# Attention energies in one PSUM bank: one scaled product, two more added on top, one exponential

## The chip, the cores and the metric

The kernel runs on one core of one Trainium2 chip. The time is the device time of one execution in microseconds (us). The kernel before took 2440.59 us (median of three runs, 2437.53 to 2440.74). The engines are PE (TensorE: matmuls and, as PEld, weight loads), ACT (ScalarE), DVE (VectorE), POOL (GpSimd, which here mostly issues DMAs) and SP (SyncE, DMAs too). SBUF is the working memory, PSUM the memory that matmuls write: 8 banks of 2 KB in each of 128 partitions.

## What is computed

Self-attention over the 4096 pixels of each of 4 images with 256 channels, without the softmax's usual subtraction of the maximum (a check of the sums at the end starts a second, general branch that the inputs here do not enter):

```
q = x @ Wq + bq ; k = x @ Wk + bk ; v = x @ Wv + bv
energy[n, m] = sum_c q[c, n] * k[c, m]          # 4096 x 4096 for each image
out[c, n]    = sum_m v[c, m] * softmax_m(energy[n, :])[m]
result       = gamma * out + x
```

The reference is in fp32. The kernel multiplies in a faster matmul type (fp32r), which keeps fewer bits, and gets the precision back by splitting each operand into a rounded upper part and remainders: three products stand for one. For the energies, with E = 2^-12, the three products (forms f = 0, 1, 2) of keys and queries are combined as (1+E)/E times the sum of the products 0 and 1, minus 1/E times product 2, and the exponential of the combination is wanted.

## The kernel before, in words

The work of an image has a **head** and 128 **steps**.

The head (loop over i = 0 to 15) makes the projections of 256 pixels at a time: `transposed` (four transposes on PE, copied out by ACT), `project_qk` (PE, then DVE adds the bias at L144; the keys are split by ACT at L263 and DVE at L266; POOL stores the queries, L275, and the split keys, L279, in DRAM) and `project_v`. From i = 10 on, `begin` slips in the energies of the first three steps, two halves (k = 0, 1) for each step.

A step u covers 512 keys and 256 queries. The order of the instructions on each engine is written out by hand in `tile_conv_attention_kernel` (a manual schedule: each engine runs its own instructions in the order of the program). In step u the program issues:

- `energy(ahead, k)` for the step that lies three ahead (LOOK = 3, ahead = u + 3), for both halves. A half is six matmuls of 128x128 weights (keys) by 256 columns (queries): forms 0 and 1 add up in the tile `sa`, form 2 goes to `sb`; each of the two tiles is one PSUM bank with two buffers. ACT takes the exponential of each (L334) into SBUF tiles `x` and `y`.
- `join(u + 2)`: DVE multiplies x by y (L344), 128x1024 elements.
- `upper(u + 2)`: ACT rounds x to its upper part h (L349). `halves(u + 1)`: DVE makes the remainders l (L355) and d (L358).
- `load_k(ahead + 2)`, L314: POOL issues the DMA of the split keys of step u + 5 (768 KB), into a pool of three buffers (`kpool`, tag "k"). So this load waits until PE has made the energies of step u + 2 out of the same buffer. POOL's other DMAs stand in the same queue: the stores of the head, and the output stores (L436).
- `attend(u)`: 24 matmuls of h, l and d of step u by three forms of the values (L398) into the tiles `a` and `bb`, which are read out every eight steps (`finish`).

So 36 matmuls make a step, 12 for energies and 24 for `attend`. The first loads of keys of an image are issued in `begin`: k_0, k_1 and k_2 at i = 4, 6 and 8, k_3 at i = 13, k_4 at i = 15; k_5 is issued in step 0. Each stands in POOL's queue behind the stores of the i before it. (k_n is the load for step n.)

Four PSUM banks hold energies (`ps_s`), three `a` and `bb` (`ps_o`), one the transposes of the result (`ps_t`).

Of the kernel before, what the change touches and what calls it, by code (L numbers as in the profile page):

```python
# [9 lines left out]
F32 = mybir.dt.float32  # L10
F32R = mybir.dt.float32r
I32 = mybir.dt.int32
AF = mybir.ActivationFunctionType
ALU = mybir.AluOpType
AX = mybir.AxisListType
PSUM = bass.MemoryType.PSUM
# [4 lines left out]
def kernel(  # L21
# [36 lines left out]
    nc = tc.nc  # L58
    B, W, H, C = x.shape
    P = 128  # L60
# [138 lines left out]
    with ExitStack() as fast:  # L199
# [10 lines left out]
        pool("pad3", 1).tile([P, 48], F32, name="pad3")  # L210
        kpool = pool("kpool", 3)
        dram = pool("dram", 2, space=DRAM)
        ps_s = pool("ps_s", 2, space=PSUM)
        ps_o = pool("ps_o", 1, space=PSUM)
        ps_t = pool("ps_t", 1, space=PSUM)

# [8 lines left out]

        images, qd, kf, units, loads, now = [], {}, {}, {}, {}, {}

        energies = cycle((ps_s, tag) for tag in "ab")
        outputs = cycle([(ps_o, "a0"), (ps_o, "a1"), (ps_o, "bb"), (ps_t, "t")])
        active = []  # L230

# [79 lines left out]
        def load_k(b, u):  # L311
            if u < STEPS:
                t = kpool.tile([P, 4, 3, P], F32R, tag="k", name=f"k_{b}_{u}")
                nc.gpsimd.dma_start(t.rearrange("p (i s) f d -> p i s (f d)", s=2), kf[b, u % NU])  # L314
                loads[b, "k", u] = t

        def energy(b, u, k):

            g, t = divmod(u, NU)
            if k == 0:  # L320
                x = ppool.tile([P, 4, NB], F32, tag="x", name=f"x_{b}_{u}", bufs=3)
                y = ppool.tile([P, 4, NB], F32, tag="y", name=f"y_{b}_{u}")
                units[b, u] = x, y
            x, y = units[b, u]
            q, kt = loads[b, "q", g], loads[b, "k", u]
            sa = ps_s.tile([P, 2, NJ, P], F32, tag="a", name=f"sa_{b}_{u}_{k}")
            sb = ps_s.tile([P, 2, NJ, P], F32, tag="b", name=f"sb_{b}_{u}_{k}")
            for i in range(2):
                for to, f, first, last in ((sa, 0, True, False), (sa, 1, False, True), (sb, 2, True, True)):
                    nc.tensor.matmul(  # L330
                        to[:, i], kt[:, 2 * k + i, f, :], q[:, f], start=first, stop=last
                    )
            for to, sp, scale in ((x, sa, (1.0 + E) / E), (y, sb, -1.0 / E)):
                nc.scalar.activation(  # L334
                    to[:, 2 * k : 2 * k + 2, :],
                    sp.rearrange("p i j d -> p i (j d)"),
                    AF.Exp,
                    scale=scale,
                )

        def join(b, u):

            x, y = units[b, u]
            nc.vector.tensor_tensor(x, x, y, ALU.mult)  # L344
            units[b, u] = x

        def upper(b, u):
            h = ppool.tile([P, 4, NB], F32R, tag="h", name=f"h_{b}_{u}", bufs=3)
# [94 lines left out]
        def finish_last(b, g, xr):  # L443

            z = zall.rearrange("p n j -> p (n j)")
            n0 = (b * NG + g) * NJ
            r = work.tile([P, 2, NJ], F32, tag="r", name=f"r_{b}_{g}")
            o = work.tile([P, NJ, C + 2], F32, tag="o", name=f"o_{b}_{g}")
            ok = ppool.tile([P, 4, NB], F32, tag="y", name="ok")
            last = ok[:, 1, : NJ + 1]  # L450
            inside(ok[:, 0, :n0], z[:, :n0])
            nc.vector.tensor_reduce(last[:, NJ:], ok[:, 0, :n0], AX.X, ALU.min)
            acc, bb = now["acc"], now["bb"]
            for j in range(NJ):
                zj, raj = z[:, n0 + j : n0 + j + 1], r[:, 1, j : j + 1]
                nc.vector.tensor_copy(zj, acc[j][:, C : C + 1])
                nc.vector.reciprocal(r[:, 0, j : j + 1], zj)  # L457
                nc.vector.tensor_tensor(raj, r[:, 0, j : j + 1], gam1, ALU.mult)
                nc.scalar.activation(o[:, j, :C], acc[j][:, :C], AF.Identity, scale=raj)
            nc.vector.tensor_tensor(r[:, 0, :], r[:, 0, :], gam.to_broadcast([P, NJ]), ALU.mult)  # L460
            inside(last[:, :NJ], z[:, n0:])

            nc.vector.tensor_reduce(zs, last, AX.X, ALU.min)
            zp = ps_s.tile([P, 1], F32, tag="b", name="zp")
            nc.tensor.matmul(zp, ones, zs, start=True, stop=True)  # L465
            tps = []
            for j in range(NJ):
                nc.vector.scalar_tensor_tensor(  # L468
                    o[:, j, :C], bb[:, j, :], r[:, 0, j : j + 1], o[:, j, :C], ALU.mult, ALU.add
                )  # L470
                tp = (ps_t, ps_s)[j].tile([P, 2, P], F32, tag="ta"[j], name=f"ot_{b}_{g}_{j}")
                for s in range(2):
                    nc.tensor.transpose(tp[:, s, :], o[:, j, s * P : (s + 1) * P], ident)  # L473
                tps.append(tp)
                if j == 0:
                    nc.vector.tensor_scalar(again, zp, P - 0.5, None, ALU.is_lt)
            for j in range(NJ):
                n = slice(j * P, (j + 1) * P)
                nc.vector.tensor_tensor(xr[:, :, n], xr[:, :, n], tps[j], ALU.add)  # L479
            nc.sync.dma_start(ov[b, g], xr)  # L480

        def begin(b, i):

            if i == 5:
                load_q(b, 0)
            if i == 9:
                for _ in halve_q(b, 0):
                    pass
            if i in (4, 6, 8):
                load_k(b, i // 2 - 2)  # L490
            if i >= 10:
                energy(b, (i - 10) // 2, i % 2)
            if i in (12, 14):
                join(b, i // 2 - 6)
            if i in (13, 15):
                upper(b, i // 2 - 6)
                load_k(b, i // 2 - 3)

        image(0)
        for b in range(B):  # L500
            pr = images[b]
            if b == 0:
                now["banks"] = energies
                pr.transposed(0)

                wp = ps_t.tile([P, P], F32, tag="t", name="wp1")
                for _ in range(2):
                    nc.tensor.matmul(wp, ones, ones, start=True, stop=True)
                pr.transposed(1)
                project_qk(b, 0)  # L510
            for i in range(1, NI):
                if i == 3:
                    now["banks"] = outputs
                if i + 1 < NI:
                    pr.transposed(i + 1)
                while i == 1 and active:
                    proceed()
                begin(b, i)
                project_qk(b, i)
                if i == NI - 1:  # L520
                    halves(b, 0)
                project_v(b, i - 1)
                proceed()
            project_v(b, NI - 1)
            for u in range(STEPS):
                g, t = divmod(u, NU)
                ahead = u + LOOK
                if ahead // NU + 1 < NG and ahead % NU == 3:
                    load_q(b, ahead // NU + 1)
                if u == STEPS - NU and b + 1 < B:  # L530
                    image(b + 1)
                if u >= STEPS - 3 and b + 1 < B:
                    now["banks"] = energies
                    if u == STEPS - 3:
                        images[b + 1].load(0)
                    elif u == STEPS - 2:
                        images[b + 1].transposed(0)
                if t == NU - 3:
                    loads[b, "x", g] = load_x(xpool, b, g)


                beside = []
                if ahead // NU + 1 < NG and ahead % NU == 5:
                    beside.append(halve_q(b, ahead // NU + 1))
                if u in (1, 3):
                    beside.append(halve_v(b, NI - 2 + u // 2))
                for k in range(2):
                    if ahead < STEPS:
                        energy(b, ahead, k)
                    if k == 0:  # L550
                        for forms in beside:
                            next(forms)
                    if k == 0 and u + 2 < STEPS:
                        join(b, u + 2)
                        upper(b, u + 2)
                load_k(b, ahead + 2)
                proceed()
                if u + 1 < STEPS:
                    halves(b, u + 1)
                for forms in beside:  # L560
                    next(forms)
                attend(b, u)
                if (b, u) == (B - 1, STEPS - 1):
                    finish_last(b, g, loads.pop((b, "x", g)))
                elif t == NU - 1:
                    start(finish(b, g, now["o"], now["bb"], loads.pop((b, "x", g))))
                proceed()
            if b + 1 < B:
                proceed()
                images[b + 1].transposed(1)  # L570
                proceed()
                project_qk(b + 1, 0)
# [135 lines left out]
```

## Time and profile before

| | |
|---|---|
| runs | 2437.53, 2440.74, 2440.59 us; median 2440.59 |
| span of the profiled execution (first to last instruction) | 2435.2 us, 5.4 below the median of the runs; no other time of that execution is given |
| granted PE clock | 0.999 of full speed |
| ACT exponentials, L334 | 2 x 1024, about 600 ns each |
| DVE multiplication, L344 | 512, 1223 ns each |
| DMA | 498.92 MB, mean 205 GB/s |

The page lists the busy time of each engine, then the costliest groups of instructions, with the mean duration of one and the idle time of the engine just before them. Matmuls overlap in PE's pipeline: a row says 277 ns for one, but successive ones start some 113 ns apart, so the spacing of starts is what counts. A DMA row tells the time from issue to landing. The waits view lists who waited for whom, and the timeline the instructions in order of time.

### The profile page before, as it was taken

The page shows a single profiled execution, that of the slowest core. Times are in us where ns is not written, and L with a number is a line of the kernel's source. Part 1 is how long each engine was busy: PE and PEld are TensorE (multiplying, and loading weights), DVE is VectorE, ACT ScalarE, POOL GpSimd, SP SyncE. Part 2 cuts the span into 40 slices and gives each one's busy share as a digit, 9 for nine tenths or more (in the row PEclk, how much of TensorE's full clock was granted, in tenths as well). Part 3 has the DMA queues.
Part 4 walks back from the last instruction along what each step waited for, and adds up shares of the span by engine and source line. Part 5 has one row for each costly group of instructions (what it writes and reads, how often), then busy time and mean ns, then how long its engine had stood idle before and what let it go on. Part 6 is the DMA issues. An engine that isn't in the chain of part 4 may idle for free.

```text
span 2435.2 us, 50041 instructions
## 1 busy us (share of the span) xinstructions
PE 2424.4 (100%) x19988; PEld 2393.4 (98%) x19988; DVE 2099.7 (86%) x2318; ACT 1795.6 (74%) x3201; POOL 424.4 (17%) x781
## 2 busy tenths in 40 slices
PE   9999999999999999999999999999999999999998
PEld 8999999999899999999989999999998999999998
DVE  5988988888698888888869888888886988888887
ACT  5777777777677777777667777777766777777775
POOL 4211111111411111111141111111114111111110
PEclk9999999999999999999999999999999999999999
DMA  7766666665776666667477666666647766666663
GB/s 234 223 204 212 206 206 202 206 215 157 232 226 198 209 208 206 210 198 214 145 242 229 202 203 209 206 212 202 206 144 245 231 204 199 211 205 213 206 203 113
DMA packets 137407, 498.92 MB, mean 205 GB/s; under 512 B 15536, under 2 KB 57264, under 8 KB 137168
## 3 DMA queue, kind: packets, MB, share of 16 engines
q0 software_dynamic: 92320, 453.17, 60.2%
q1 hardware_dynamic: 44304, 42.22, 5.6%
q8 instruction: 160, 2.62, 0.4%
q14 instruction: 79, 0.65, 0.1%
q10 hardware_dynamic: 544, 0.26, 0.0%
HBM read 445.25 MB, written 50.33 MB: 204 GB/s over the span
## 4 chain that ended last, share of the span: by engine, by line
PE 99%; DMA 0%; DVE 0%; SPq 0%; issue 0%
PE a L398 40%; PE bb L398 19%; PE sa L330 19%; PE sb L330 10%; PE qk L135 5%; PE v L156 5%; PE xt L122 1%; PE ot L431 1%; DMA x<-in_x_dram 0%; SPq L82 0%; DVE o L468 0%; PE ot L473 0%; DVE x L479 0%; PE zp L465 0%; DVE r L457 0%
## 5 line engine op out<-in xcount | busy, mean ns | idle before, releaser
L334 ACT ACTIVATE x<-sa 128x512 f32<-128x512 f32 x1024 | 612.6, 598 | 498.9 <-PE sa L330 494.9
L344 DVE TENSOR_TENSOR x<-x,y 128x1024 f32<-128x1024 f32 x512 | 626.4, 1223 | 218.5 <-ACT y L334 218.5
L330 PE MATMUL sa<-q,k 128*128 128x256 f32 x4096 | 733.5, 279 | 0.0
L358 DVE SCALAR_TENSOR_TENSOR d<-h,x 128x1024 fp32r<-128x1024 f32 x512 | 623.5, 1218 | 0.0
L355 DVE TENSOR_TENSOR l<-x,h 128x1024 fp32r<-128x1024 f32 x512 | 623.3, 1217 | 0.0
L330 PEld LDWEIGHTS sa<-q,k 128*128 128x128 f32 x4096 | 617.9, 188 | 0.7 <-ACT x L334 0.2
L334 ACT ACTIVATE y<-sb 128x512 f32<-128x512 f32 x1024 | 616.6, 602 | 0.0
L398 PE MATMUL a<-vh,h 128*128 128x258 f32 x4096 | 569.7, 281 | 0.0
L398 PE MATMUL a<-vl,l 128*128 128x258 f32 x4096 | 568.9, 281 | 0.0
L330 PE MATMUL sb<-q,k 128*128 128x256 f32 x2048 | 566.3, 277 | 0.0
L398 PE MATMUL bb<-vd,d 128*128 128x256 f32 x4096 | 553.1, 277 | 0.0
L349 ACT ACTIVATE h<-x 128x1024 fp32r<-128x1024 f32 x512 | 543.9, 1062 | 9.1 <-DVE x L344 8.9
L314 POOL DMA_DIRECT2D k<-kf x512 | 279.1, 545 | 1558.0 <-PE sb L330 1529.6
L398 PEld LDWEIGHTS a<-vl,l 128*128 128x128 f32 x4096 | 521.9, 189 | 0.0
L398 PEld LDWEIGHTS a<-vh,h 128*128 128x128 f32 x4096 | 519.3, 189 | 0.0
L398 PEld LDWEIGHTS bb<-vd,d 128*128 128x128 f32 x4096 | 509.9, 188 | 0.0
L330 PEld LDWEIGHTS sb<-q,k 128*128 128x128 f32 x2048 | 385.0, 188 | 0.1
L135 PE MATMUL qk<-wqk_sb,xts 128*128 128x256 f32 x512 | 121.1, 379 | 0.0
L156 PE MATMUL v<-xts,wv_sb 128*128 128x256 f32 x512 | 120.3, 379 | 0.0
L156 PEld LDWEIGHTS v<-xts,wv_sb 128*128 128x128 f32 x512 | 97.3, 190 | 13.2
L135 PEld LDWEIGHTS qk<-wqk_sb,xts 128*128 128x128 f32 x512 | 92.3, 190 | 10.0
L275 POOL DMA_DIRECT2D qd<-qks x128 | 69.2, 549 | 178.4 <-DVE qks L144 169.0
(60 smaller groups left out, 868.0 us busy)
## 6 DMA issues: line engine op xcount, KB each, us to landing
k<-kf POOLq DMA_DIRECT2D x512, 768.0 KB, 4.6
x<-in_x_dram SPq DMA_DIRECT2D x128, 256.0 KB, 4.0
kf<-f POOLq DMA_DIRECT2D x64, 384.0 KB, 3.9
out_dram<-x POOLq DMA_DIRECT2D x63, 256.0 KB, 2.6
qd<-qks POOLq DMA_DIRECT2D x128, 64.0 KB, 2.9
qr<-qd SPq DMA_DIRECT2D x64, 128.0 KB, 3.7
wv_sb<-in_L_conv_Wv_dram POOLq DMA_DIRECT2D x1, 256.0 KB, 6.5
out_dram<-x SPq DMA_DIRECT2D x1, 256.0 KB, 3.4
```

The costliest lines, as they stand in the source:

```text
L122: nc.tensor.transpose(tp[:, k, s, :], self.xs[i][:, s, k * P : (k + 1) * P], ident,)
L135: nc.tensor.matmul(qk[:, s, :], self.xt[i][:, k, s, :], wqk_sb[:, k, :], start=(k == 0), stop=(k == KC - 1),)
L156: nc.tensor.matmul(vp[:, eh, :], wv_sb[:, k, eh * P : (eh + 1) * P], self.xt[i][:, k].rearrange("p s a -> p (s a)"), start=(k == 0), stop= ...
L275: nc.gpsimd.dma_start(qd[b, i // 2 + NG // 2 * s][:, i % 2, :], x[:, s, :C2])
L314: nc.gpsimd.dma_start(t.rearrange("p (i s) f d -> p i s (f d)", s=2), kf[b, u % NU])
L330: nc.tensor.matmul(to[:, i], kt[:, 2 * k + i, f, :], q[:, f], start=first, stop=last)
L334: nc.scalar.activation(to[:, 2 * k : 2 * k + 2, :], sp.rearrange("p i j d -> p i (j d)"), AF.Exp, scale=scale,)
L344: nc.vector.tensor_tensor(x, x, y, ALU.mult)
L349: nc.scalar.activation(h, units[b, u], AF.Identity, scale=UPPER)
L355: nc.vector.tensor_tensor(l, x, h.bitcast(F32), ALU.subtract)
L358: nc.vector.scalar_tensor_tensor(d, h.bitcast(F32), 1.0 + E, x, ALU.mult, ALU.subtract)
L398: nc.tensor.matmul(out_, left[:, i, j * P : (j + 1) * P], right[:, m, : out_.shape[1]], start=(t == 0 and bank not in begun), stop=(t == N ...
```

## The change

Each half's energies use one PSUM bank, tag "e", of which there are now four buffers. `cross` makes form 2's two matmuls into it and ACT multiplies the bank in place by -1/(1+E); later `energy` adds forms 0 and 1 on top of it (their matmuls do not start a new sum), and one exponential with scale (1+E)/E reads it. The tile `y` and `join` go. Since `energy` can only add after ACT's scaling, `cross` is called one step earlier than `energy`: in step u the program issues `cross(ahead + 1)` for both halves, then `energy(ahead)`. In the head the two calls are spread over i = 10 to 15.

```diff
-        ps_s = pool("ps_s", 2, space=PSUM)
+        ps_s = pool("ps_s", 4, space=PSUM)
...
+        def chunk(b, u, k, f, first):
+
+            g, t = divmod(u, NU)
+            q, kt, e = loads[b, "q", g], loads[b, "k", u], units[b, "e", u, k]
+            for i in range(2):
+                nc.tensor.matmul(
+                    e[:, i],
+                    kt[:, 2 * k + i, f, :],
+                    q[:, f],
+                    start=first and i == 0,
+                    stop=(f == 1),
+                    skip_group_check=True,
+                )
+
+        def cross(b, u, k):
+
+            if u >= STEPS:
+                return
+            e = units[b, "e", u, k] = ps_s.tile([P, 2, NJ, P], F32, tag="e", name=f"e_{b}_{u}_{k}")
+            chunk(b, u, k, 2, True)
+            nc.scalar.mul(e, e, -1.0 / (1.0 + E))
+
         def energy(b, u, k):
...
+            for f in range(2):
+                chunk(b, u, k, f, False)
             if k == 0:
-                x = ppool.tile([P, 4, NB], F32, tag="x", name=f"x_{b}_{u}", bufs=3)
-                y = ppool.tile([P, 4, NB], F32, tag="y", name=f"y_{b}_{u}")
...
+            nc.scalar.activation(
+                units[b, u][:, 2 * k : 2 * k + 2, :],
+                units.pop((b, "e", u, k)).rearrange("p i j d -> p i (j d)"),
+                AF.Exp,
+                scale=(1.0 + E) / E,
+            )
-        def join(b, u):
-
-            x, y = units[b, u]
-            nc.vector.tensor_tensor(x, x, y, ALU.mult)
-            units[b, u] = x
...
             if i >= 10:
-                energy(b, (i - 10) // 2, i % 2)
-            if i in (12, 14):
-                join(b, i // 2 - 6)
+                for c in ("", "0", "1", "23", "4", "5")[i - 10]:
+                    energy(b, int(c) // 2, int(c) % 2)
+                for c in ("01", "2", "3", "45", "6", "7")[i - 10]:
+                    cross(b, int(c) // 2, int(c) % 2)
...
                 for k in range(2):
-                    if ahead < STEPS:
-                        energy(b, ahead, k)
+                    cross(b, ahead + 1, k)
+                for k in range(2):
+                    energy(b, ahead, k)
...
                     if k == 0 and u + 2 < STEPS:
-                        join(b, u + 2)
                         upper(b, u + 2)
```

A digit c in `begin` stands for step c // 2, half c % 2. The places of `load_k` in the program are not changed. Three small tiles at the end of the last image move from the tags "y", "a" and "b" to "x" and "e".

More of the change, by code (lines that the diff above doesn't have):

```diff
@@ L226 @@
         images, qd, kf, units, loads, now = [], {}, {}, {}, {}, {}
-        energies = cycle((ps_s, tag) for tag in "ab")
+        energies = cycle([(ps_s, "e")])
         outputs = cycle([(ps_o, "a0"), (ps_o, "a1"), (ps_o, "bb"), (ps_t, "t")])
@@ L317, in energy @@
+        def cross(b, u, k):
[4 more added lines that the diff above has]
+            nc.scalar.mul(e, e, -1.0 / (1.0 + E))
         def energy(b, u, k):
-            g, t = divmod(u, NU)
+            if u >= STEPS:
+                return
+            for f in range(2):
+                chunk(b, u, k, f, False)
             if k == 0:
-                x = ppool.tile([P, 4, NB], F32, tag="x", name=f"x_{b}_{u}", bufs=3)
-                y = ppool.tile([P, 4, NB], F32, tag="y", name=f"y_{b}_{u}")
-                units[b, u] = x, y
@@ L324, in energy @@
-            x, y = units[b, u]
[L325 to L339, printed above, removed]
-        def join(b, u):
-            x, y = units[b, u]
-            nc.vector.tensor_tensor(x, x, y, ALU.mult)
-            units[b, u] = x
+                units[b, u] = ppool.tile([P, 4, NB], F32, tag="x", name=f"x_{b}_{u}", bufs=3)
@@ L448, in finish_last @@
             o = work.tile([P, NJ, C + 2], F32, tag="o", name=f"o_{b}_{g}")
-            ok = ppool.tile([P, 4, NB], F32, tag="y", name="ok")
+            ok = ppool.tile([P, 4, NB], F32, tag="x", name="ok", bufs=3)
             last = ok[:, 1, : NJ + 1]
@@ L463, in finish_last @@
             nc.vector.tensor_reduce(zs, last, AX.X, ALU.min)
-            zp = ps_s.tile([P, 1], F32, tag="b", name="zp")
+            zp = ps_s.tile([P, 1], F32, tag="e", name="zp")
             nc.tensor.matmul(zp, ones, zs, start=True, stop=True)
@@ L470, in finish_last @@
                 )
-                tp = (ps_t, ps_s)[j].tile([P, 2, P], F32, tag="ta"[j], name=f"ot_{b}_{g}_{j}")
+                tp = (ps_t, ps_s)[j].tile([P, 2, P], F32, tag="te"[j], name=f"ot_{b}_{g}_{j}")
                 for s in range(2):
```

## The prediction, made before the changed kernel ran

> **What bounds the kernel now.** I read the page first: the busy shares and the chain that ended last.
>
> ```profile
> PE 2424.4 (100%) x19988; PEld 2393.4 (98%) x19988; DVE 2099.7 (86%) x2318; ACT 1795.6 (74%) x3201; POOL 424.4 (17%) x781
> ...
> PE 99%; DMA 0%; DVE 0%; SPq 0%; issue 0%
> ```
>
> PE is the chain from the first microseconds to the last. A change in ACT or DVE alone can then give nothing; it can only take, by making PE wait. So next I read who waits today.
>
> ```profile
> POOL k L314 <- PE sb L330: 1529.6, 427, 3.9
> ACT x L334 <- PE sa L330: 494.9, 492, 1.6
> DVE x L344 <- ACT y L334: 218.5, 416, 0.7
> ...
> PEld sa L330 <- ACT x L334: 0.2, 1, 0.2
> ```
>
> Everybody waits for PE, and PE for almost nobody. The first row matters most: each load of keys waits on POOL until PE frees a buffer, so the loads cannot be issued earlier than they are. Third, the timeline at the end of the first image's head and in its first steps:
>
> ```profile
> 60.38 0.54 POOL L279 DMA_DIRECT2D kf<-f  x1 [0.39 <-issue]
> ...
> 60.91 0.55 POOL L314 DMA_DIRECT2D k<-kf  x1
> ...
> 63.42 0.48 PE L330 MATMUL sa<-q,k 128*128 128x256 f32 x2
> ...
> 70.11 0.56 POOL L314 DMA_DIRECT2D k<-kf  x1
> ...
> 73.37 0.59 PE L330 MATMUL sa<-q,k 128*128 128x256 f32 x2
> ...
> 73.87 0.56 POOL L314 DMA_DIRECT2D k<-kf  x1
> ...
> 75.43 0.54 POOL L314 DMA_DIRECT2D k<-kf  x1 [1.00 <-PE sb L330]
> ...
> 77.80 0.39 PE L330 MATMUL sa<-q,k 128*128 128x256 f32 x2
> ...
> 79.62 0.53 POOL L314 DMA_DIRECT2D k<-kf  x1 [3.65 <-PE sb L330]
> ```
>
> The rows of L314 issue k_3, k_4, k_5, k_6, k_7; 63.42 is i = 14, 73.37 is step 0, 77.80 step 1. Today k_3 is first needed in step 0, k_4 in step 1 and so on. Asked for L314 in windows of the trace, the landing times from issue are these, first for the loads of this window, then for those of 100 to 600 us:
>
> ```profile
> DMA to landing us min/median/max: 5.3/6.2/7.1
> ```
>
> ```profile
> DMA to landing us min/median/max: 4.3/4.6/7.4
> ```
>
> **PE's work.** Six matmuls a half before, six after: 6144 in all, same weights, same columns. In the timeline the energies start 113 ns apart (301.86, 302.20 three later) whether the next one adds to the same bank, to another half of it or changes bank. So the new order of forms costs nothing by these rows: 0.
>
> **ACT.** 1024 exponentials of y (L334, 602 ns) become 1024 scalings of PSUM in place. The trace has no write to PSUM by ACT; nearest are a plain copy out of PSUM of the same size (L128, 569 ns), the exponential itself (602 ns) and, in SBUF alone, L292 (128x512, 630 ns) and half of L349 (531 ns). I take 0.60 us, the row that reads the same banks; at 0.53 or 0.63 nothing below changes. Back to back, ACT starts one every 0.48 us (303.12 to 303.60), and L349's h takes 0.94 (299.41 to 300.35). A step is 4.17 us and asks 4 x 0.48 + 0.94 = 2.86 us of ACT. Written out from a step's start: the first bank's two matmuls are done at 0.11 + 0.31 = 0.42 (0.31 from last start to ACT's start, as at 302.31 to 302.62); scalings to 1.38, first exponential to 1.86, h to 2.80, second exponential to 3.40. The next step's third matmul wants that bank at 4.17 + 0.23 = 4.40. That leaves 1.0 us; the two L423 instructions (0.53 us each, once in eight steps) use it up but do not pass it. Cost 0. The scaled bank is needed only a step later: some 3 us to spare.
>
> **DVE.** 512 multiplications (L344, 1.22 us) go: 626 us of busy time. Its cover is complete, since PE never waited for DVE in the steps; so the gain is 0, and l is the next thing late on DVE, with most of a step in hand.
>
> **The loads.** Here is the cost. Form 2 of step u + 4 is multiplied in step u, so k_n is needed one step (4.17 us) sooner, while its issue stays: the buffer is still freed by the last energy matmul of step n - 6, and POOL's queue is as before (stores, then the load). PE's `cross` stands ahead of everything in its step; behind it wait the step's other 34 matmuls.
>
> In the steps: issue 1.82 us after the start of step n - 6 (79.62 against 77.80), need at the start of step n - 4: 2 x 4.17 - 1.82 = 6.5 us. The median landing is 4.6, the longest 7.4. I compared each of the 484 loads from k_7 on, landing against the end of `attend(n - 5)` in the trace of before: 14 come late, by 5.3 us together (0.85, 0.69, 0.66 the longest; four of these places belong to a load that POOL issued a whole step late, once in each stretch of about 620 us). With 0.1 us for the release, 14 x 0.1 + 5.3 = **6.7 us**.
>
> In the heads, image 0:
> - k_3, first needed at i = 14. By the start of i = 14 PE has made 28 instead of 24 energy matmuls, so i = 14 starts 4 x 0.113 = 0.45 later, and `cross` comes after `energy`'s four: 63.42 + 0.45 + 0.45 = 64.3. The load is issued sooner, because DVE at i = 12 no longer has the multiplication in front of the bias (L144 at 57.94 behind L344 at 56.81): 1.2 us, so 59.7; landing 59.7 + 5.3 = 65.0. PE waits 0.7, with the release 0.8 (1.9 if DVE's relief does not reach POOL's queue).
> - k_4, needed at the start of step 0: 73.37 + 0.45 + the wait before. Its issue hangs on PE's own queries of i = 14 (POOL stores them first), so it moves with the same wait, less what L344 at 66.01 no longer blocks: 70.11 + 0.45 + wait - 1.1. Need minus landing: 73.82 - (69.46 + 5.5) = -1.1. PE waits 1.1, with the release **1.2**, whatever k_3 did.
> - k_5: issue shifted to about 74.7 (behind the stores of i = 15), needed at step 1's start, 80.2. Landing took 6.8, with k_6 beside it; k_6 now goes out later, after step 0's energies. Between 5.5 (as k_4) and 6.8 it waits 0 to 1.3; I take 0.5, nearer the uncontended row.
> - k_6 has 6.5 us as in the steps, and k_5's wait besides: 0.
>
> The other heads have the same spacing. In image 2 k_3 took 6.2 (+0.9), in image 1 k_4 took 7.5 and k_5 8.2 (+2.0 for k_4, which then leaves k_5 in time). This is where PE waits today already, for k_4 landing at 682.36:
>
> ```profile
> 681.39 1.08 PE L398 MATMUL bb<-vd,d 128*128 128x256 f32 x8
> ...
> 682.50 0.47 PE L330 MATMUL sa<-q,k 128*128 128x256 f32 x2
> ```
>
> Heads: k_3 4 x 0.8 + 0.9 = 4.1; k_4 4 x 1.2 + 2.0 = 6.8; k_5 3 x 0.5 = 1.5; **12.4 us**.
>
> **The sum.** 12.4 + 6.7 - 0.2 (the wait of image 1, counted already) = 19 us; I say 18.5, since some of the late loads follow each other. Span 2435.2 + 18.5 = 2453.7; the runs' median lies 5.4 above the span: **2459 us**. Bounds of the unknowns: heads 5 (k_5 at 0, k_3 and k_4 issued half a microsecond sooner) to 25 (k_3 at 1.9, k_5 at 1.3, a slow load in each head), steps 0 to 12 (the slow landings fall elsewhere in each run).
>
> **Rivals.**
> 1. *No change: the loads come in time after all.* This needs landings about 1.2 us shorter, as could be if DVE's work holds up POOL's DMAs. For it: the scale of DVE's relief. Against it: the issue takes 0.53 us throughout, and the landings are longest in the heads (5.3 to 7.1), where DVE has 5 to 6 tenths, and 4.6 in the steps, where it has 8. Then the k_3 and k_4 waits fall to 0 and the steps' to 1 or 2: +2, 2442 us. [...]
> 2. *Faster: PE's spacing falls.* The matmuls of `attend` start 119 ns apart for a (303.21 to 304.17 for eight), and the first of bb 116 to 119, the last 113. If DVE's traffic stretched them, 30% less of it would free something on each of 24 x 512 = 12288 matmuls: a nanosecond is 12.3 us, and from 1.9 ns on (23.4 us) the kernel is faster by over 0.2%. At 2.5 ns it is 2435.2 + 18.5 - 31 + 5.4 = 2428. Against it: energies stand at 113 beside the same L355, and in the 28 places where neither ACT nor DVE runs beside a, the spacing is 118.7.
> 3. *Slower still: ACT's writes into PSUM disturb PE.* The nearest rows: bb's matmuls are 115 to 116 apart beside ACT's PSUM reads of y, 113.4 without: 2.5 ns. The two scalings cover some 10 matmuls a step: 10 x 2.5 x 512 = 13 us more, 2472.
> 4. *It doesn't do what it says:* a scaled bank that ACT delivers late would make PE wait each step; the ACT sum above leaves 3 us, so I give it nothing of its own.
>
> **How the numbers follow.** The forecast (late loads, +10 to +30) has 0.66, the first rival 0.17, the second 0.07, the third 0.10. 0.2% of this kernel is 5 us, about what a measurement of it can tell from no change. Faster than 2435.7: the second rival, 0.07. Within 5 us: the first, and a little of the forecast's low end, 0.18. Slower: 0.75. The range from 2445 to 2474 takes in the forecast's bounds and most of the third rival; 2 in 10 lie outside, in the first two.
>
> **What would show it.** Waits of PE in the profile of the changed kernel: rows "PE e <- DMA k<-kf", some 8 to 12 in the heads of 0.5 to 3 us each, about a dozen short ones in the steps; none for ACT. DVE about 1475 us busy, ACT's scalings 0.53 to 0.63 us. If PE waits for ACT, the ACT sum is wrong; if the spacing of `attend` moves, one of rivals 2 and 3; if the heads cost under 5 us, the landings were mis-sized.

## The result, and the profile after

The changed kernel took 2457.72 us (median, 2454.75 to 2458.21), the kernel before 2439.85 us beside it: a ratio of 1.0072, 95% interval 1.0058 to 1.0086. The profiled execution's span is 2452.9 us, 17.7 us more than the 2435.2 of before.

The page of the changed kernel: busy times, the chain that ended last by engine, and some of its groups.

```profile
PE 2429.7 (99%) x19988; PEld 2394.9 (98%) x19988; DVE 1523.2 (62%) x1806; ACT 1799.7 (73%) x3201; POOL 424.3 (17%) x781
...
PE 91%; DMA 4%; issue 2%; ACT 1%; DVE 1%; POOL 1%; SPq 0%; POOLq 0%; DVEq 0%; ACTq 0%
...
L337 ACT ACTIVATE e<-e 128x512 f32<-128x512 f32 x1024 | 549.6, 580 | 507.7 <-PE e L322 507.6
...
L322 PE MATMUL e<-q,k 128*128 128x256 f32 x6144 | 794.7, 278 | 11.6 <-DMA k<-kf 10.2
...
L347 ACT ACTIVATE x<-e 128x512 f32<-128x512 f32 x1024 | 621.9, 608 | 5.5 <-issue 5.5
L405 PE MATMUL a<-vh,h 128*128 128x258 f32 x4096 | 569.7, 281 | 0.0
L405 PE MATMUL a<-vl,l 128*128 128x258 f32 x4096 | 568.9, 281 | 0.0
L405 PE MATMUL bb<-vd,d 128*128 128x256 f32 x4096 | 553.0, 277 | 0.0
```

DVE lost 576 us of work and ACT's total rose by only 4; the time rose all the same. The busy time of the `attend` matmuls is what it was, to 0.1 us. New is the wait of the energies' matmuls for the loads of keys, and it cuts into a chain that was 99% PE: it now runs through DMA, POOL and the head's ACT and DVE work too. Who waits for whom, of the changed kernel:

```profile
POOL k L314 <- PE e L322: 1554.6, 428, 5.1
ACT e L337 <- PE e L322: 507.6, 495, 2.7
...
PEld e L322 <- issue: 11.0, 12, 2.9
PE e L322 <- DMA k<-kf: 10.2, 14, 2.5
```

No row has PE waiting for ACT's scaling. (One wait for k_4, in image 2, the view puts down to ACT's copy of the values, L165; k_4 landed 0.14 us before PE went on, as in every other wait for keys.) The 10.2 us understate the loss, since a matmul's row, 278 ns long where starts are 113 apart, ends some 0.17 us after the next one could have started; so I read the loss from the starts of successive matmuls: how much later than usual the two matmuls after a wait start. One such place, the first steps of image 0 (timeline of the changed kernel):

```profile
70.49 0.54 POOL L279 DMA_DIRECT2D kf<-f  x1 [0.39 <-issue]
...
71.02 0.56 POOL L314 DMA_DIRECT2D k<-kf  x1
...
72.00 3.62 PE L156 MATMUL v<-xts,wv_sb 128*128 128x256 f32 x16
...
75.48 0.56 POOL L314 DMA_DIRECT2D k<-kf  x1
...
76.33 1.62 PE L322 MATMUL e<-q,k 128*128 128x256 f32 x12 [0.71 <-DMA k<-kf]
...
79.71 1.08 PE L405 MATMUL bb<-vd,d 128*128 128x256 f32 x8
...
81.65 1.62 PE L322 MATMUL e<-q,k 128*128 128x256 f32 x12 [0.86 <-DMA k<-kf]
```

The last matmul of the projections starts at 75.24 and the energies could follow at 75.27; k_4, issued at 71.02 behind the stores of i = 14, lands at 76.20, and PE goes on at 76.33. At 80.6 `attend(0)` is done, and k_5 lands at 81.51. Adding up all such gaps in the starts:

| place | predicted | measured |
|---|---|---|
| k_3, four heads | 4.1 | 0.67 + 0.61 + 0.70 + 0.88 = 2.9 |
| k_4 | 6.8 | 0.97 + 2.75 + 1.21 + 1.13 = 6.1 |
| k_5 | 1.5 | 1.10 + 0 + 0.55 + 1.43 = 3.1 |
| steps | 6.7 (14 waits) | 4.2 (13 waits, 0.06 to 1.27) |
| first `cross` of an image waits for its queries | - | 0.9, less 0.4 that was there before |
| first load of pixels, at the very start | - | 0.8 later than before |
| image 1's wait, gone elsewhere | -0.2 | -0.3 |

(For k_4, 0.1 of each gap is left out, which PE took at that place before the change too.) The sum is 17.3, and the spans differ by 17.7. Loads of keys make 16.0 of it (2.9 + 6.1 + 3.1 + 4.2 - 0.3).

### The profile page after: what moved, and what is told of

Same layout as the page of the kernel before. It is cut to its first block, busy times and chain, and to the rows that moved or that the text cites. A ratio compares the mean times of both kernels' runs of the same rounds, so it can differ in the third digit from the quotient of the medians.

```text
span 2452.9 us, 50094 instructions
## 1 busy us (share of the span) xinstructions
PE 2429.7 (99%) x19988; PEld 2394.9 (98%) x19988; DVE 1523.2 (62%) x1806; ACT 1799.7 (73%) x3201; POOL 424.3 (17%) x781
## 4 chain that ended last, share of the span: by engine, by line
PE 91%; DMA 4%; issue 2%; ACT 1%; DVE 1%; POOL 1%; SPq 0%; POOLq 0%; DVEq 0%; ACTq 0%
PE a L405 38%; PE e L322 28%; PE bb L405 18%; DMA k<-kf 3%; PE qk L135 3%; PE v L156 2%; PE ot L438 1%; DMA kf<-f 1%; PE xt L122 1%; ACT v L165 0%; DVE qks L144 0%; DVE f L266 0%; ACT f L263 0%; DMA x<-in_x_dram 0%; ACT vh L292 0%
## 5 line engine op out<-in xcount | busy, mean ns | idle before, releaser
L337 ACT ACTIVATE e<-e 128x512 f32<-128x512 f32 x1024 | 549.6, 580 | 507.7 <-PE e L322 507.6
L322 PE MATMUL e<-q,k 128*128 128x256 f32 x6144 | 794.7, 278 | 11.6 <-DMA k<-kf 10.2
L322 PEld LDWEIGHTS e<-q,k 128*128 128x128 f32 x6144 | 738.7, 188 | 16.4 <-issue 11.0
L347 ACT ACTIVATE x<-e 128x512 f32<-128x512 f32 x1024 | 621.9, 608 | 5.5 <-issue 5.5
L442 DVE TENSOR_TENSOR x<-x,ot 128x512 f32<-128x512 f32 x63 | 43.3, 687 | 185.8 <-PE ot L438 185.8
L423 DVE COPY zall<-o 128x2 f32<-128x2 f32 x63 | 10.7, 170 | 160.2 <-ACT o L417 160.2
L263 ACT ACTIVATE f<-qks 128x256 fp32r<-128x256 f32 x64 | 26.7, 418 | 74.9 <-DVE qks L144 69.5
```

What stands on the lines that cost most here:

```text
L322: nc.tensor.matmul(e[:, i], kt[:, 2 * k + i, f, :], q[:, f], start=first and i == 0, stop=(f == 1), skip_group_check=True,)
L337: nc.scalar.mul(e, e, -1.0 / (1.0 + E))
L347: nc.scalar.activation(units[b, u][:, 2 * k : 2 * k + 2, :], units.pop((b, "e", u, k)).rearrange("p i j d -> p i (j d)"), AF.Exp, scale=(1 ...
L442: nc.vector.tensor_tensor(xr, xr, tp, ALU.add)
```

## The experiments

The theory on trial: the whole loss is PE waiting for loads of keys that are wanted a step sooner than they were, while their issue did not move. The rivals: the scaling in PSUM or the new order of the matmuls costs PE something; DVE's work bears on the DMAs.

### A fourth buffer for the loads

```diff
-                t = kpool.tile([P, 4, 3, P], F32R, tag="k", name=f"k_{b}_{u}")
+                t = kpool.tile([P, 4, 3, P], F32R, tag="k", name=f"k_{b}_{u}", bufs=4)
```

> The changed kernel with a fourth buffer for the loads of keys, and nothing else. Theory (the whole loss is PE waiting for loads of keys that are needed a step sooner): in the steps a load is then issued a step (4.2 us) sooner, and the dozen waits there (4.2 us in the profile of the changed kernel) go; the heads keep theirs (12.4 us), since their loads stand behind stores in POOL's queue, buffers or not. k_5 may wait somewhat longer, as k_6 comes beside it. Time 2453 to 2456 us, 1.005 to 1.007 of before; waits left in the profile only for k_3, k_4, k_5 of each image. Rival (ACT's work in PSUM or the new order of matmuls stretches PE): no wait of the steps matters, time as the changed kernel, 2458, with the spacing of matmuls over 1 ns wider than before. Rival (loads slow each other): more loads in flight, landings longer, waits in the steps stay.

2454.45 us, 1.0062 (1.0048 to 1.0076), in the range given. The heads kept 11.2 of their 12.1 us for k_3, k_4, k_5, as foreseen. The steps did not become free: four waits of 0.2 to 1.2 us remain, 2.5 us together, and each is for the load that follows an output store in POOL's queue (loads 16 and 40 of image 1, 16 of image 2, 64 of image 3). A buffer more lets POOL run ahead, but a store of the output that waits for DVE stands in the same queue. POOL's rows ahead of the wait for load 16 of image 1:

```profile
731.09 0.69 POOL L443 DMA_DIRECT2D out_dram<-x  x1 [7.63 <-DVE x L442]
731.67 1.19 POOL L314 DMA_DIRECT2D k<-kf  x2
```

POOL stands still for 7.6 us, and two loads go out together behind the store. So the waits of the steps shrank from 4.2 to 2.5 us, less than the theory said. The times can't tell this gain from none: the changed kernel's interval is 1.0058 to 1.0086.

### Four buffers and the loads of the head sooner

Beside the fourth buffer:

```diff
-            if i in (4, 6, 8):
+            if i in (4, 6, 8, 10):
                 load_k(b, i // 2 - 2)
...
+            if i in (13, 14):
+                load_k(b, i - 9)
...
-                load_k(b, ahead + 2)
+                load_k(b, ahead + 3)
```

> As the one before, and the loads of the head issued sooner: k_3 at i = 10, k_4 at i = 13, k_5 at i = 14, and in step u the load of step u + 6. Each load then has at least the time before its first use that it had before the change. Theory: no wait of PE for keys is left, neither in heads nor steps: 12.4 + 4.2 = 16.6 us less than the changed kernel, span about 2436, time 2439 to 2442, 0.999 to 1.001 of before. Rival (ACT's scaling in PSUM or the order of matmuls costs part of the loss): stays above 1.002, by the part that the loads do not explain.

2439.27 us, 0.9999 (0.9990 to 1.0008), span 2435.7. The page and all waits of its energies' matmuls:

```profile
PE 2424.0 (100%) x19988; PEld 2393.3 (98%) x19988; DVE 1522.7 (63%) x1806; ACT 1798.6 (74%) x3201; POOL 424.5 (17%) x781
```

```profile
PEld e L322 <- DVE q L266: 0.6, 1, 0.6
PE e L322 <- DVE q L266: 0.4, 1, 0.4
```

No wait for keys is left, and with it the whole loss is gone, though form 2, the scaling in place, the order of the matmuls and the relief of DVE are all still there. This is the run that decides: what the change does on ACT, in PSUM and on DVE costs nothing and gives nothing here. The one row left is the first `cross` of an image, which asks for the form of the queries that DVE makes last.

### Form 2 in the same step

In the steps, `energy` moves behind `attend`; in the head, `begin` calls `cross` alone and `energy` stands behind `project_qk`:

```diff
                 for k in range(2):
-                    cross(b, ahead + 1, k)
+                    cross(b, ahead, k)
                 for k in range(2):
-                    energy(b, ahead, k)
...
                 attend(b, u)
+                for k in range(2):
+                    energy(b, ahead, k)
...
             if i >= 10:
-                for c in ("", "0", "1", "23", "4", "5")[i - 10]:
-                    energy(b, int(c) // 2, int(c) % 2)
-                for c in ("01", "2", "3", "45", "6", "7")[i - 10]:
-                    cross(b, int(c) // 2, int(c) % 2)
+                cross(b, (i - 10) // 2, i % 2)
...
                 project_qk(b, i)
+                if i >= 10:
+                    energy(b, (i - 10) // 2, i % 2)
```

> The changed kernel with three buffers, but form 2 made in the same step as forms 0 and 1: at the start of step u the four matmuls of form 2 for step u + 3, then attend(u), then the eight matmuls of forms 0 and 1 for step u + 3; in the head form 2 ahead of the projection of queries and keys and the others behind it. Keys are then needed in the step in which they were needed before the change; the buffer is freed at the step's end, 2.8 us later than before, with 8.2 us from issue to need. Theory: no waits in the steps (longest landing 7.4), heads as before: 2438 to 2443 us, 0.999 to 1.002. Rival (scaling in place is itself the cost, since PE must wait for ACT or is disturbed by its writes): ACT has attend's 2.8 us for two scalings of 0.55, so a wait for ACT would show as PE rows released by ACT, and the time would stay at 2455 or rise above it.

2454.69 us, 1.0064 (1.0050 to 1.0078): the theory missed. The steps did what it said (two waits, 0.8 us in all). The heads lost 3 to 4 us each in another way. Waits and timeline of this run, at i = 12 of image 0:

```profile
PEld e L322 <- ACT e L337: 16.7, 24, 1.6
...
PE e L322 <- ACT e L337: 4.4, 5, 1.2
```

```profile
59.02 0.48 PE L322 MATMUL e<-q,k 128*128 128x256 f32 x2
...
59.34 1.89 PE L135 MATMUL qk<-wqk_sb,xts 128*128 128x256 f32 x8
59.73 0.63 ACT L292 ACTIVATE vh<-v 128x512 fp32r<-128x512 f32 x1
60.27 0.57 ACT L128 COPY xts<-xt 128x512 f32<-128x512 f32 x1
...
60.73 0.59 ACT L337 ACTIVATE e<-e 128x512 f32<-128x512 f32 x1
...
61.38 0.74 PE L322 MATMUL e<-q,k 128*128 128x256 f32 x4
```

Form 2 is done at 59.4; ACT first has the roundings and copies of the head in front of it, comes to the scaling at 60.73 and ends at 61.32. PE has only the projection of queries and keys to do meanwhile, and could go on some 0.4 us sooner, by its starts. So the rival's wait exists, where the cover is 1.7 us and ACT's queue is full.

### The same, with more cover in the head

As in the run before, but in the head `energy` stands behind `project_v`:

```diff
                 project_v(b, i - 1)
+                if i >= 10:
+                    energy(b, (i - 10) // 2, i % 2)
```

> As the run with form 2 in the same step, but in the head forms 0 and 1 stand behind the projection of the values too, 1.7 us later. There PE waited 0.3 us (and 0.1 more in each case) for ACT's scaling in nearly every i from 10 on, 1.3 us at the first, because ACT reaches it behind the copies and roundings of the head. Theory: the loss of that run is those waits alone, some 3 to 4 us an image; with 1.7 us more of cover they go, and with three buffers the kernel is back at 2439 to 2443, 0.999 to 1.0015. Rival (keeping forms 0 and 1 behind attend costs something in the steps): stays above 1.003 with waits of PE in the steps.

2440.76 us, 1.0003 (0.9994 to 1.0012). No wait for ACT's scaling is left; in the steps there are two for keys, of 0.3 us each, and two heads wait 0.5 and 0.7 us for ACT's copy of the values (L165). With three buffers as before, the one-bank form is as fast as the kernel before, if form 2 is not drawn a step forward.

### The loads of the head sooner, three buffers

```diff
-                load_k(b, i // 2 - 3)
+            if i in (12, 14, 15):
+                load_k(b, {12: 3, 14: 4, 15: 5}[i])
...
-                load_k(b, ahead + 2)
+                if u:
+                    load_k(b, ahead + 2)
```

> The changed kernel with three buffers, where in the heads alone the loads are issued sooner: k_3 at i = 12, k_4 at i = 14, k_5 at i = 15, each as soon as its buffer is free; the steps are as in the changed kernel. Theory: the heads' 12.4 us go (at most 1 us is left), the dozen waits of the steps stay with 4 to 5 us: 2443 to 2446, 1.0015 to 1.003. Together with the fourth buffer alone, which took only the steps' part, this splits the loss in two. Rival (heads and steps share one cause, the number of buffers): the waits of the heads stay, 2455 or more.

2443.98 us, 1.0021 (1.0012 to 1.0030). None of the waits of the heads for keys is left; in the steps eight remain, 2.5 us in the profile. Of the change's 18 us three quarters were thus lost in four stretches of some 15 us each, because k_3, k_4 and k_5 of each image stood where they did in POOL's queue.

### Two buffers in the kernel before

```diff
-                t = kpool.tile([P, 4, 3, P], F32R, tag="k", name=f"k_{b}_{u}")
+                t = kpool.tile([P, 4, 3, P], F32R, tag="k", name=f"k_{b}_{u}", bufs=2)
...
-            if i in (4, 6, 8):
+            if i in (4, 6):
...
-                load_k(b, i // 2 - 3)
+            if i in (12, 14, 15):
+                load_k(b, {12: 2, 14: 3, 15: 4}[i])
```

> The kernel before the change, its two exponentials and its product, with two buffers for the loads of keys instead of three (in the head k_2, k_3, k_4 are issued at i = 12, 14 and 15). In the steps a load then has the same 6.5 us from issue to need as in the changed kernel; in the head each has more than it took. Theory: PE waits a dozen times in the steps, 4 to 7 us together, and hardly in the heads: 2443 to 2448 us, 1.002 to 1.003 of before, waits released by loads of keys though nothing of the change is in it. Rival (the loss belongs to the accumulation in one bank or to the scaling in place): as before, 0.999 to 1.001, no waits.

2447.96 us, 1.0037 (1.0023 to 1.0050). Nothing of the change is in this kernel, yet taking 4.2 us from the loads' slack brings the same waits: 13 in the steps, 4.8 us together by the starts, each ended by a load's landing. The waits view has the longer ones, and the windows view (columns: time, PE, weight loads, DVE, ACT, POOL, PEclk for the granted clock, DMA share, GB/s) shows one thing more, at the start:

```profile
PE sa L330 <- DMA k<-kf: 2.2, 5, 1.0
```

```profile
8.00:11.40 3.40, 2.85 (x9) 2.50 (x10) 0.00 (x0) 0.59 (x1) 0.22 (x1) 0.50 0.62 188
```

The span of this profile is 7.7 us above that of before: 5.0 are waits for keys (0.2 of them in a head), 1.8 a later landing of the first pixels (PE waits 2.9 for them, 1.1 before), and 0.9 the first projections behind that wait, whose matmuls start 427 ns apart and not 216, with the granted clock at half. The profiles of the other experiments begin as slowly, for 1 to 3 us of their spans, except the deciding one (four buffers and early loads); the changed kernel's does not either.

### Two buffers in the changed kernel

> The changed kernel with two buffers for the loads of keys instead of three (in the head k_2, k_3 and k_4 are issued behind the energies that free their buffers, at i = 12, 13 and 15). Theory: in the steps a load goes out 1.82 us into step n - 5 and is wanted at the start of step n - 4, 2.35 us later; with a landing of 4.6 and 0.1 for the release PE waits 2.4 us in some 490 steps: +1150 us, 3550 to 3700, with PE's granted clock unchanged and every wait released by a load of keys. Rival (the loss of the changed kernel comes from something else and the slack of the loads is not what decides): far less, under 2600. Rival (waits of some 2 us in every step lower PE's clock, so waits compound): granted clock clearly under 0.99 and more than 4000 us.

The edit is `bufs=2` in `load_k`, with k_2, k_3 and k_4 issued at i = 12, 13 and 15. 3761.96 us, 1.5423 (1.5394 to 1.5451): 62 us above the range given, so the theory missed in part. The page:

```profile
PE 2704.1 (72%) x19988; PEld 2584.2 (69%) x19988; DVE 1533.5 (41%) x1806; ACT 1808.1 (48%) x3201; POOL 425.2 (11%) x781
...
L322 PE MATMUL e<-q,k 128*128 128x256 f32 x6144 | 934.7, 306 | 1046.5 <-DMA k<-kf 1046.1
```

The slack sum gave 2.4 us of wait in some 490 steps, 1150 us; measured from the starts it is 2.2 in the middle (the median) and 1114 us in all. So issue, landing and need, read off the trace, foretell a wait of this size within a few per cent. The span grew by 214 us more. Some 160 of them are PE's clock, by an estimate: half of the 321 us in which it was granted at half speed before the last matmul (below). Another 40 or so are the second matmul after each wait, which starts 0.08 us later than usual. The theory had the clock unchanged; the rival with the clock was right that it falls (0.956) and wrong on the size.

### DVE's multiplication put back, its result unused

```diff
+        def join(b, u):
+
+            y = ppool.tile([P, 4, NB], F32, tag="y", name=f"y_{b}_{u}")
+            nc.vector.tensor_tensor(y, units[b, u], units[b, u], ALU.mult)
...
+            if i in (12, 14):
+                join(b, i // 2 - 6)
...
+                        join(b, u + 2)
                         upper(b, u + 2)
```

> The changed kernel with VectorE's multiplication put back where it stood, as a square of x into a tile that nobody reads (the result of the kernel is the same; 512 x 1.22 us of VectorE are wasted). Theory: VectorE's relief brought k_3 forward by 1.2 us in each head, by way of the bias addition and the stores in front of it in POOL's queue; with the product back, PE waits 1.2 us longer for k_3 in each image, and 0 to 1.1 longer for k_4: +5 to +9 us on the changed kernel, 2462 to 2467, 1.009 to 1.011 of before; nothing else moves. Rival (VectorE's work holds up POOL's DMAs or PE): landings of the loads in the steps get longer and the waits there grow too. Rival (VectorE does not matter at all): as the changed kernel, 2458.

2461.36 us, 1.0086 (1.0072 to 1.0100), 0.6 below the range given. The waits for k_3 grew from 2.9 to 6.9 us (1.65, 1.69, 1.71, 1.83), 1.0 each; those for k_4 (6.2) and k_5 (2.2) and those of the steps (3.5) did not grow. At i = 14 of image 0, timeline of this run:

```profile
67.83 0.72 PE L322 MATMUL e<-q,k 128*128 128x256 f32 x4
69.95 0.48 PE L322 MATMUL e<-q,k 128*128 128x256 f32 x2 [1.41 <-DMA k<-kf]
```

So DVE's relief did help: it spared k_3 about 4 us, by way of the bias addition and POOL's queue, and not by making any DMA faster (k_3 landed 5.1 to 5.4 us after its issue in both). As the other waits were 1.5 us shorter in this profile, all waits for keys grew by 2.5 us. The times alone do not show the difference, since the intervals of the two kernels overlap.

## Why the prediction was right, step by step

*PE's work costs nothing.* Right. In the changed kernel the energies start 113 ns apart as before, and the groups of `attend` are busy for the same time (above); the run with four buffers and early loads has before's time with all of the new order in it. That settles the rivals *faster by spacing* and *slower by ACT's writes*: beside a scaling in PSUM (`e<-e`) the starts of energies are 113 ns apart in the median, as they are beside no work of ACT, and those of `attend` did not come closer (118 ns in the median, before and after) with 27% less of DVE.

*ACT.* The scaling in place was priced at 0.60 us from the row that reads the same bank; it took 580 ns, between the plain copy (569) and the exponential (608). No wait of PE for ACT's scaling in the changed kernel, as the sum said. The wait that the text weighed and put aside is real where the cover is short: in the run with form 2 in the same step.

*DVE's multiplication gives nothing by itself.* Right but for the path that the text named, 1.2 us for each k_3; measured 1.0. The busy time fell by 576 us and not by the 626 of L344, since neighbouring instructions overlap (before, a multiplication starts at 301.47 for 1.22 us and l at 302.61): the rows of DVE add up to 123 us more than its busy time before and to 78 more after.

*The loads.* The mechanism, the places and the sum were right (18.5 predicted, 17.7 measured in the span), but the parts were less so, and the sum gained from their errors going both ways: the loads alone cost 16.0, and 1.3 came from the first pixels and the queries, which the text did not have. The steps' waits were 4.2 us where 6.7 was taken: 13 for 14, and eight of the 13 are for loads that the trace of before had named, among them the four that POOL issued a step late. k_3 was 1.2 us less, because in image 2 the landing took 5.2 this time and not 6.2. k_5 was 1.6 more: the text took its wait near the uncontended landing of 5.5, and it took 5.7 to 6.5, near the other end, though k_6 went out 2.8 us behind it instead of 1.6. Image 1's slow k_4 (7.5 before, 6.7 after) came again and made the longest wait, 2.8 us.

*From span to time.* The 5.4 us that the text added were taken as fixed. The profiled run of the changed kernel took 2454.75 us, 1.9 above its own span, and in all later runs the two also lie 1.7 to 1.9 apart. The rest is that this profile fell on the fastest of its runs; by the same 1.8, that of before belongs to a run of 2437.0 us, at the fast end of its runs too. The median came out 4.8 above the span; that it lay so near 5.4 again is luck.

*The rival "no change".* Out: landings in the steps have a median of 4.6 before and after, with DVE at 86% and at 62%. With 512 `tensor_tensor` instructions less the median stayed at 4.6, and with them put back it was 4.6 too (4.58, 4.57 and 4.63 over the loads from k_7 on).

## What to carry to other kernels

Where an engine is busy from end to end, ask of a change first what it makes that engine want sooner: for each load whose first use moves, write down issue, landing and need, in the steady loop and at the seams, where the load stands in a queue behind stores that its need does not wait for. Work taken off an engine that nobody waits for is worth only what stands behind it in some queue. If the first use must move, the issue has to move with it, by a buffer more and by its place in the queue; both were needed here (the buffer alone left 1.0062, the place alone 1.0021), and then the version was as fast as before and no faster.

## What the runs showed of the hardware that was not expected

PE's clock fell with waits of some 2 us in every step. In the run with two buffers in the changed kernel the granted clock was 0.956 over the span, and 0.999 in the changed kernel; the trace has 92 stretches at half speed, 330 us together, most of them some 3.4 us long (the last, of 9 us, lies at the end, where the trace of before has one of 8.0 and that of the changed kernel one of 8.3). The windows view of three `attend`s, with PEclk as the granted clock (all columns: time, PE, weight loads, DVE, ACT, POOL, PEclk, DMA share, GB/s):

```profile
500.00:503.30 3.30, 3.30 (x18) 3.30 (x17) 0.00 (x0) 2.00 (x4) 0.53 (x1) 0.53 0.43 114
506.78:509.70 2.92, 2.92 (x26) 2.79 (x24) 0.77 (x1) 2.11 (x4) 0.53 (x1) 1.00 0.39 88
513.70:517.00 3.30, 3.30 (x18) 3.30 (x18) 0.00 (x0) 1.93 (x3) 0.53 (x1) 0.54 0.48 112
```

The same matmuls take 1.9 us for eight in the first and third, 1.1 in the second. The timeline has PE waiting 0.90 us for keys ahead of the second and 2.29 ahead of the third. By the starts of this run, after waits of 0.5 to 2 us none of 92 steps was slow in its first eight matmuls of `attend`, after 2.0 to 2.5 us 13% of 295 were, after more than 3 us 10 of 16.

Half speed also followed a single wait: at the start of the run with two buffers in the kernel before, PE waited 2.9 us for the first pixels, and from 8.0 to 11.4 us the granted clock was 0.50. The longest wait of the changed kernel, 2.8 us, was followed by none (1.00 in the 5.2 us from 686.80). So the length of a wait does not settle it alone; what else does was not shown.
